# Shift products on two row tiles, set-up transfers from another engine, and other figures for the planner: a fused convolution and attention kernel

## The chip, the cores and the metric

The kernel runs on one core of a Trainium2 chip. The metric is the device time of one execution in microseconds; the kernel before took 4647.31 us (median of 3 runs, 4646.46 to 4648.82). The profiled execution spans 4642.4 us from its first to its last instruction.

A core has engines that work side by side, each through its own list of instructions in order: TensorE (PE in the profile, with its weight loads as PEld), VectorE (DVE), ScalarE (ACT), GpSimd (POOL) and SyncE (SP), which here only issues transfers. An instruction waits for semaphores that other engines and transfers raise; everything behind it on its engine waits with it.

## The reference

The input is 32 images of 96 channels and 56 x 56 pixels. Cut to what is computed:

```python
# layer 0, per image
h = relu(bn(w1 @ x))                  # 96 -> 576 channels
h = relu(bn(depthwise_conv3x3(h)))    # 9 taps a channel
x = x + bn(w2 @ h)                    # 576 -> 96 channels, and the residual
# layer 1, on 3136 tokens of 96 channels
u = relu(bn(layernorm(t) @ w1.T))     # 96 -> 192
X = fft(u)                            # over the tokens
y = ifft(relu(Re(X*c) + rb) + 1j * relu(Im(X*c) + ib)).real
t = t + bn(y @ w2.T)
t = t + ffn(layernorm(t))             # 96 -> 384 -> 96, rounded to fp8 and fp16
```

The batch norm behind `w2` is a scale, which the kernel multiplies into `w2`, and a shift of one number a channel, which has to be added to every token.

## The kernel before

**Stages.** An image is cut into two halves of 28 rows. For each half the 576 channels are worked as four blocks of 128 (`unit`, L598) and one of 64 (`last_channels`, L702). A unit expands on TensorE (L615), ScalarE evicts with Relu into `hs` (L625), begins the depthwise sum `acc` with one tap (L641) and makes one or two products (L657); VectorE adds the other taps (L668); GpSimd issues transfers that add the products to `acc` (L676); ScalarE finishes with a Relu (L685). `front` (L863) then brings everything to tokens: for 14 blocks of 112 tokens it sums in PSUM the transposed residual (L881, `ident`), the products with `w2T` over four channel blocks (L881), those of the last channels (L915), and the shift (L897). ScalarE evicts to `xt` (L928), and SyncE stores it (L937) for later. A layer norm on VectorE, a projection and a first transform follow (L974 to L1037); `mid` (L1067) does the Fourier mixing, and `back` (L1286) the inverse transform (L1324), the addition to the residual (L1329), the second norm, and the fp8 network (L1345 to L1458).

**The shift products.** `shb` holds the shift as three bf16 rows whose sum is the fp32 number, written four times side by side; `ones` is 3 x 112 ones. A product of `ones` and `shb` over a contraction of 3 adds the shift to four blocks of tokens at once. `front` walks two token halves t = 0, 1, which lie in two PSUM banks of the tile `pw`: for each t it issues four (or three) transposes and then one shift product. An image has four such pairs.

**The set-up.** `second` (L476) computes the shift on VectorE early in the kernel and sends each of the three rows to its partition of `shb` with a transfer issued by ScalarE (L484). `attention`, `mixer` and `ffn` prepare the other stages' constants; their square roots run on ScalarE (L432). SyncE issues the loads.

**The order.** No order is written out by hand. Each piece of work is a `step` with an engine, a cost, steps it comes after, buffers it takes and gives back, and a rank, the time at which it is due (`START`, `PACE`, `OFF`, `AT`). `Plan.emit` (L222) plays the engines forward on a clock of its own: an idle engine takes the due step of lowest rank whose inputs are ready and whose buffers are free. A step counts as done for others at its cost plus `late`, by engine from `LATE` (L163) or given. What comes out is the order of each engine's instructions, fixed at build time. `OFF[3]` is the rank of the finishing Relu within its unit.

**Fillers.** TensorE's clock falls when it idles. Where the planner's TensorE has nothing to do and was busy for less than 75% of the last 3.4 planned microseconds (`sparse`, L194), it issues a product of `ident` with itself into an unused part of `pw` (L1486), and charges 0.23 us. Such a product stands in TensorE's order like any other. An fp32 product shows as two passes in the trace.

**The buffers.** Three PSUM tiles `ps` serve all stages but `front`, which has `pw`; `acc` has seven buffers, `al` two, `product` and `hs` three each.

Of the kernel before, what the change touches and what calls it, by code (L numbers as in the profile page):

```python
# [34 lines left out]
BF16 = mybir.dt.bfloat16  # L35
# [6 lines left out]
C = 96  # L42
# [13 lines left out]
G = 7  # L56
# [74 lines left out]

SPARSE = 0.75
FILLER = 0.23

OFF = (-4.5, 0.5, 0.5, 8.5)
AT = (3.0, 0.5)

DOUBLE = (1, 3)
# [15 lines left out]
class Plan:  # L154
# [5 lines left out]

    LATE = {"PE": 0.23, "ACT": 0.18, "DVE": 0.15}  # L163
    WINDOW = 3.413
    LITTLE, FULL = 0.58, 0.965

# [55 lines left out]
    def emit(self):  # L222
        ready = {s.engine: [] for s in self.steps}
        idle = dict.fromkeys(ready, True)
        for s in self.steps:
            if not s.left:
                heapq.heappush(ready[s.engine], (s.rank, s.at, s))
        events, count, left = [(0.0, 0, None, None)], 1, len(self.steps)
        work = sum(s.engine == "PE" for s in self.steps)
        while events:  # L230
            now = events[0][0]
            while events and events[0][0] <= now:
                _, _, engine, s = heapq.heappop(events)
                if engine:
                    idle[engine] = True
                elif s:
                    for b in s.give:
                        self.free[b] += 1
                    for n in s.next:
                        n.left -= 1  # L240
                        if not n.left:
                            heapq.heappush(ready[n.engine], (n.rank, n.at, n))
            for engine, heap in ready.items():
                if not idle[engine]:
                    continue
                passed, wanted = [], set()
                while heap:
                    item = heapq.heappop(heap)
                    s = item[2]
                    short = {b for b in s.take if self.free[b] < s.take.count(b)}  # L250
                    if short or wanted.intersection(s.take):
                        wanted |= short
                        passed.append(item)
                        continue
                    for b in s.take:
                        self.free[b] -= 1
                    s.emit()
                    left -= 1
                    idle[engine] = False
                    cost = self.stretched(now, s.cost) if engine == "PE" else s.cost  # L260
                    if engine == "PE":
                        self.recent.append((now, now + cost))
                        work -= 1
                    late = self.moved(now, s.late) if isinstance(s.late, tuple) else s.late
                    heapq.heappush(events, (now + cost, count, engine, None))
                    heapq.heappush(events, (now + cost + late, count + 1, None, s))
                    count += 2
                    break
                for item in passed:
                    heapq.heappush(heap, item)  # L270
                if engine == "PE" and idle[engine] and work and now > 0 and self.sparse(now):

                    self.filler()
                    idle[engine] = False
                    cost = self.stretched(now, FILLER)
                    self.recent.append((now, now + cost))
                    heapq.heappush(events, (now + cost, count, engine, None))
                    count += 1
        assert not left, "a step waits for a buffer that nothing frees"
# [3 lines left out]
def tile_kernel(ctx: ExitStack, tc: tile.TileContext, d: dict, out: bass.AP):  # L283
# [19 lines left out]
    def cst(shape, name, dt=F32):  # L303
        return const.tile(shape, dt, name=name, tag=name)
# [29 lines left out]
    bd = cst([128, NK + 1], "bd")  # L334
    m2rb = cst([128, 2], "m2rb")

    shb = cst([3, 4, C], "shb", BF16)
    ones = cst([3, SK], "ones", BF16)
    w1q = cst([C, HF], "w1q", F8)
    w2q = cst([128, 3, C], "w2q", F8)  # L340
    b1q = cst([128, 3], "b1q")
# [134 lines left out]
    def second():  # L476
        g, v, b, m = given[0]
        s = scale_of(g, v, 128, C)
        sh, rest = tmp(1, C), tmp(1, C)
        shift_of(sh, b, m, s[0:1, :], rest)  # L480
        for n in range(3):
            part = tmp(1, 4 * C, BF16)
            nc.vector.tensor_copy(part.rearrange("p (q c) -> p q c", q=4), sh.unsqueeze(1).to_broadcast([1, 4, C]))
            nc.scalar.dma_start(out=shb[n : n + 1, :, :].rearrange("p q c -> p (q c)"), in_=part)  # L484
            nc.vector.tensor_sub(rest, sh, part[:, 0:C])
            sh = rest
        nc.vector.tensor_mul(w2T, w2T, s.unsqueeze(1).to_broadcast([128, NK + 1, C]))
# [66 lines left out]
    def pe(n, m, passes):  # L554
        return passes * max(0.855 * n, 0.88 * m) / 1000
# [307 lines left out]
    def front(img, s):  # L863
# [5 lines left out]
        def conv(i):  # L869

            def f():
                if i == 0:
                    if s == 0:

                        ydr[img] = dram.tile([2, NP, S, HA], F32, name="ydr", bufs=4)

                        tdr[img] = dram.tile([2, SK, RP * C], F32, name="tdr", bufs=4)
                    u["t"] = w1.tile([SK, RP, C], F32, name="xt")

                def add(n, t, src, rhs, rows=slice(None), **k):  # L880
                    nc.tensor.matmul(  # L881
                        u["pw"][0:SK, t, n % 4, 0:C],
                        lhsT=src[rows, (G * t + n) * SK : (G * t + n + 1) * SK],
                        rhs=rhs,
                        skip_group_check=True,
                        **k,
                    )

                if i % 4 == 0:
                    u["pw"] = pw[:, :, 0 : 4 * C].rearrange("p t (q c) -> p t q c", c=C)  # L890
                    n = min(4, G - i)

                    for t in range(2):
                        for m in range(i, i + n):
                            src = xs[img, s][:, x0 : x0 + W]
                            add(m, t, src, ident[0:C, 0:C], start=(m == i), stop=False, is_transpose=True)
                        nc.tensor.matmul(  # L897
                            u["pw"][0:SK, t, 0:n, 0:C],
                            lhsT=ones,
                            rhs=shb[:, 0:n, :],  # L900
                            start=False,
                            stop=False,
                            skip_group_check=True,
                        )
                for t in range(2):
                    for k in range(NK):
                        src = acc[img, s, k].rearrange("p r c -> p (r c)")
                        add(i, t, src, w2T[:, k, :], start=False, stop=False)
                if i in (3, 6):

                    last = acc[img, s, NK].rearrange("p r c -> p (r c)")
                    for n in range(i - i % 4, i + 1):
                        for t in range(2):
                            rows = slice(64 * t, 64 * t + 64)
                            nc.tensor.matmul(  # L915
                                u["pw"][0:SK, t, n % 4, 0:C],
                                lhsT=last[rows, n * SK : (n + 1) * SK],
                                rhs=w2T[rows, NK, :],
                                start=False,
                                stop=True,  # L920
                                skip_group_check=True,
                            )

            return f
# [15 lines left out]
        ev = []  # L940
        for i in range(G):
            n = min(4, G - i) if i % 4 == 0 else 0
            cost = pe(C, SK, 16) + n * (pe(C, SK, 2) + 0.13)
            if i in (3, 6):
                cost += pe(C, SK, 2 * (i % 4 + 1))
            t = [
                step(
                    "PE",
                    cost,
                    conv(i),  # L950
                    t,
                    ["pw"] * (i % 4 == 0) + ["xt"] * (i == 0) + ["ydr", "tdr"] * (s == 0 and i == 0),
                    (["acc"] * 4 + ["al"]) * (i == G - 1),
                )
            ]
            if i in (3, 6):
                a = i - i % 4
                ev.append(step("ACT", act((i + 1 - a) * 2 * C), evict(a, i + 1), t, [], ["pw"]))
# [327 lines left out]
    def back(img, h):  # L1286
# [41 lines left out]
        def add():  # L1328
            nc.vector.tensor_add(u["t"], u["t"], slots(u["ps"])[0:SK, 0:G, 0:C])  # L1329

        t = step("PE", pe(C, SK, 2 * G), spread, loads + [res], ["ps"], ["wd", "gd"])
        t = step("DVE", dve(G * C, 0.06), add, [t], [], ["ps"])
        t = norm(u, "f", G, SK, [t], True, NF, [])

# [219 lines left out]
```

## Time and profile before

| engine | busy us | share of the span | instructions |
|---|---|---|---|
| TensorE, products | 4496.0 | 97% | 35608 |
| TensorE, weight loads | 3351.9 | 72% | 35608 |
| VectorE | 4335.3 | 93% | 7053 |
| ScalarE | 4121.2 | 89% | 5390 |
| GpSimd | 339.9 | 7% | 397 |

| group | executions | busy us | mean ns |
|---|---|---|---|
| L668, taps, VectorE | 1664 | 2972.6 | 1793 |
| L615, expansion, TensorE | 2048 | 805.3 | 515 |
| L881, products with w2T, TensorE | 7168 | 792.8 | 264 |
| L1486, fillers, TensorE | 1862 | 268.2 | 283 |
| L897, shift products (n = 4), TensorE | 128 in the group | 46.7 | 365 |

The first table adds over the whole execution, so it averages a start, a steady state and a tail. The mean of a product in the second is a latency: products overlap, so busy time divided by the number (0.144 us for a pass of a filler) or, better, the distance of two starts says what one occupies. The transfers move 170 GB/s on average, and the granted TensorE clock is 0.994 over the execution.

### The profile page before, as it was taken

What the parts mean: (1) busy time and instruction counts of PE and PEld (TensorE: products, weight loads), DVE (VectorE), ACT (ScalarE), POOL (GpSimd) and SP (SyncE); (2) the same over time, 40 slices, a digit from 0 to 9 for tenths busy, and PEclk for the clock granted to TensorE, in tenths of its full rate; (3) what the DMA queues carried; (4) which work ended last, traced back from release to release, by engine and by line L of the source; (5) the groups of instructions that cost most, each with busy time, mean ns of one, the idle gap of its engine ahead of it and who ended that gap; (6) DMA issues with size and microseconds to landing.
All of it is one profiled execution on the core that took longest, in us unless ns stands there. A gap on an engine that the chain in (4) does not pass through costs nothing.

```text
span 4642.4 us, 89413 instructions
## 1 busy us (share of the span) xinstructions
PE 4496.0 (97%) x35608; PEld 3351.9 (72%) x35608; DVE 4335.3 (93%) x7053; ACT 4121.2 (89%) x5390; POOL 339.9 (7%) x397
## 2 busy tenths in 40 slices
PE   7999999999999999999999999999999999999998
PEld 4667777777777777777777777777777777777777
DVE  7899999999999999999999999999999999999956
ACT  4677999999999999999999999999999999999854
POOL 0100000000000000000000000000000000000000
PEclk8999999999999999999999999999999999999999
DMA  3577877767877777777767877767776867877753
GB/s 78 130 160 174 192 168 179 183 166 181 187 170 171 187 168 179 185 174 171 184 165 181 187 169 171 187 167 180 187 172 171 187 165 179 191 170 171 170 148 100
DMA packets 390902, 789.51 MB, mean 170 GB/s; under 512 B 135600, under 2 KB 236532, under 8 KB 390484
## 3 DMA queue, kind: packets, MB, share of 16 engines
q1 hardware_dynamic: 335028, 479.15, 37.0%
q0 software_dynamic: 55296, 304.64, 34.1%
q8 instruction: 280, 4.59, 0.4%
q14 instruction: 138, 1.13, 0.1%
q10 hardware_dynamic: 160, 0.01, 0.0%
HBM read 286.38 MB, written 192.68 MB: 103 GB/s over the span
## 4 chain that ended last, share of the span: by engine, by line
PE 56%; ACT 14%; DVE 14%; DMA 5%; issue 3%; SPq 0%; DVEq 0%; ACTq 0%; POOLq 0%
PE pw L881 14%; PE ps L615 9%; DVE acc L668 7%; PE ps L1118 4%; PE ps L1031 3%; PE ps L1000 3%; PE ps L1324 3%; ACT product L657 3%; DMA acc<-product 3%; PE ps L1216 2%; PE ps L753 2%; PE ps L1378 2%; PE pw L915 2%; PE ps L1423 2%; PE ps L717 1%
## 5 line engine op out<-in xcount | busy, mean ns | idle before, releaser
L668 DVE SCALAR_TENSOR_TENSOR acc<-hs,wdw,acc 128x1540 f32<-128x1540 f32 (+2 forms) x1664 | 2972.6, 1793 | 30.1 <-ACT acc L641 22.1
L615 PE MATMUL ps<-xs,w1T 96*128 96x406 f32 x2048 | 805.3, 515 | 18.7 <-ACT hs L625 13.7
L881 PEld LDWEIGHTS pw<-w2T,acc 128*112 128x112 f32 x7168 | 749.4, 178 | 63.6 <-issue 44.5
L881 PE MATMUL pw<-w2T,acc 128*112 128x96 f32 x7168 | 792.8, 264 | 0.5 <-ACT acc L685 0.5
L657 ACT ACTIVATE product<-hs,wdw 128x1568 f32<-128x1568 f32 (+1 forms) x384 | 609.4, 1588 | 17.8 <-DMA product<-product 17.4
L625 ACT ACTIVATE hs<-ps,b 128x812 f32<-128x812 f32 x512 | 478.7, 935 | 114.9 <-PE ps L615 85.1
L615 PEld LDWEIGHTS ps<-xs,w1T 96*128 96x128 f32 x2048 | 363.1, 191 | 251.2 <-issue 177.4
L676 POOL DMA_DIRECT2D acc<-product x256 | 224.6, 877 | 3317.1 <-DVE rf L854 936.7
L641 ACT ACTIVATE acc<-hs,bd,wdw 128x1568 f32<-128x1568 f32 x256 | 435.4, 1701 | 0.2
L685 ACT ACTIVATE acc<-acc 128x1568 f32<-128x1568 f32 x256 | 387.5, 1514 | 42.8 <-DMA acc<-product 42.6
L753 PE MATMUL ps<-hl,band 128*64 128x385 f32 (+3 forms) x3072 | 416.0, 495 | 0.2 <-ACT gc L1258 0.2
L1000 PE MATMUL ps<-watt,xnT 97*120 97x192 f32 x1792 | 334.1, 330 | 16.7 <-DVE V L1147 13.4
L1000 PEld LDWEIGHTS ps<-watt,xnT 97*120 97x120 f32 x1792 | 292.5, 183 | 71.9 <-issue 35.8
L1118 PEld LDWEIGHTS ps<-wb,yb 112*128 112x128 f32 x3528 | 296.6, 165 | 52.2 <-issue 16.0
L1390 ACT ACTIVATE h<-ps 128x784 f16<-128x784 f32 x384 | 315.5, 824 | 15.4 <-PE ps L1378 10.1
L1405 ACT ACTIVATE h<-h 128x784 fp8e5<-128x784 f16 x348 | 298.8, 859 | 34.0 <-DVE h L1396 33.7
L1118 PE MATMUL ps<-wb,yb 112*128 112x112 f32 x3528 | 321.2, 270 | 5.8 <-ACT h L1390 2.5
L1345 ACT ACTIVATE u<-tt,mf,rf 112x96 fp8e5<-112x96 f32 x812 | 315.2, 463 | 0.6 <-DVE mf L857 0.6
L753 PEld LDWEIGHTS ps<-hl,band 128*64 128x64 f32 (+1 forms) x3072 | 152.2, 134 | 209.9 <-issue 180.0
L1486 PE MATMUL pw<-ident 128*128 128x128 f32 x1862 | 268.2, 283 | 3.4 <-ACT xt L928 3.4
L1486 PEld LDWEIGHTS pw<-ident 128*128 128x128 f32 x1862 | 247.4, 197 | 24.9 <-issue 12.5
L1396 DVE TENSOR_SCALAR h<-h,b1q 128x784 f16<-128x784 f16 x384 | 160.2, 418 | 83.9 <-ACT h L1390 81.9
(170 smaller groups left out, 6788.0 us busy)
## 6 DMA issues: line engine op xcount, KB each, us to landing
acc<-product POOLq DMA_DIRECT2D x256, 784.0 KB, 7.3
product<-product POOLq DMA_DIRECT2D x128, 756.0 KB, 10.6
yb<-ydr SPq DMA_DIRECT2D x252, 294.0 KB
wd<-in_wd_dram SPq DMA_DIRECT2D x128, 349.1 KB
wb<-in_wb_dram SPq DMA_DIRECT2D x63, 686.0 KB
ydr<-ya SPq DMA_DIRECT2D x256, 168.0 KB
xs<-in_x_dram SPq DMA_DIRECT2D x64, 609.0 KB
tdr<-xt SPq DMA_DIRECT2D x64, 588.0 KB
```

The costliest lines, as they stand in the source:

```text
L615: nc.tensor.matmul(u[h][:, j, 0:QW], lhsT=w1T[:, 128 * k : 128 * (k + 1)], rhs=xs[img, s][0:C, at : at + QW], start=True, stop=True,)
L625: nc.scalar.activation(flat[:, 2 * h * QW : 2 * (h + 1) * QW].rearrange("p (j w) -> p j w", j=2), u[h][:, :, 0:QW], AF.Relu, bias=b1[:, k ...
L641: nc.scalar.activation(acc[img, s, k], u["hs"][:, o + up : o + up + R, :], AF.Identity, scale=weight(up, 0), bias=bd[:, k : k + 1],)
L657: nc.scalar.activation(u["p", dr][:, ra:rb, :], u["hs"][:, ra + o + dr : rb + o + dr, :], AF.Copy, scale=weight(dr, 0))
L668: nc.vector.scalar_tensor_tensor(dst, src, weight(dr, dc), dst, ALU.mult, ALU.add)
L685: nc.scalar.activation(acc[img, s, k], acc[img, s, k], AF.Relu)
L753: nc.tensor.matmul(pv[:, :, ca:cb], lhsT=band[rows, j, dc + 1, 64 * o : 64 * o + 64], rhs=H[rows, q : q + 7, ca + dc : cb + dc], skip_grou ...
L881: nc.tensor.matmul(u["pw"][0:SK, t, n % 4, 0:C], lhsT=src[rows, (G * t + n) * SK : (G * t + n + 1) * SK], rhs=rhs, skip_group_check=True, **k,
L1000: nc.tensor.matmul(pv[0:PK, q - a, 0:HA], lhsT=xnT[:, q, 0:PK], rhs=watt, start=True, stop=True,)
L1118: nc.tensor.matmul(o, lhsT=lhsT, rhs=u["wb"][:, G * s + q, :], start=True, stop=True)
L1390: nc.scalar.activation(u["h", c].rearrange("p (j w) -> p j w", j=2), u["H", c][:, :, 0:n], AF.Copy)
L1486: nc.tensor.matmul(pw[:, 0, 4 * C :], lhsT=ident, rhs=ident, start=False, stop=False, skip_group_check=True)
```

## The change

It does three things. The two shift products of a group are issued next to each other after the transposes of both halves, and take their operands from different rows: `ones` and `shb` become 67 rows high with a second copy at rows 64 to 66, so that the product of t = 0 uses the row tile at 0 and that of t = 1 the one at 64. The transfers that fill `shb` are now six and are issued by GpSimd. And the planner gets other figures: TensorE results count as later (0.30 in place of 0.23, and 0.40 for the spread at L1324), the shift products as cheaper, the finishing Relu is due half a unit of rank earlier, and no filler is issued before its clock shows 15.

```diff
+FIRST = 15.0
-OFF = (-4.5, 0.5, 0.5, 8.5)
+OFF = (-4.5, 0.5, 0.5, 8.0)
...
-    LATE = {"PE": 0.23, "ACT": 0.18, "DVE": 0.15}
+    LATE = {"PE": 0.3, "ACT": 0.18, "DVE": 0.15}
...
-                if engine == "PE" and idle[engine] and work and now > 0 and self.sparse(now):
+                if engine == "PE" and idle[engine] and work and now > FIRST and self.sparse(now):
...
-    shb = cst([3, 4, C], "shb", BF16)
-    ones = cst([3, SK], "ones", BF16)
+    shb = cst([67, 4, C], "shb", BF16)
+    ones = cst([67, SK], "ones", BF16)
...
-            nc.scalar.dma_start(out=shb[n : n + 1, :, :].rearrange("p q c -> p (q c)"), in_=part)
+            for o in (n, 64 + n):
+                nc.gpsimd.dma_start(out=shb[o : o + 1, :, :].rearrange("p q c -> p (q c)"), in_=part)
...
                         for m in range(i, i + n):
                             src = xs[img, s][:, x0 : x0 + W]
                             add(m, t, src, ident[0:C, 0:C], start=(m == i), stop=False, is_transpose=True)
+                    for t in range(2):
+                        rows = slice(64 * t, 64 * t + 3)
                         nc.tensor.matmul(
                             u["pw"][0:SK, t, 0:n, 0:C],
-                            lhsT=ones,
-                            rhs=shb[:, 0:n, :],
+                            lhsT=ones[rows, :],
+                            rhs=shb[rows, 0:n, :],
...
-            cost = pe(C, SK, 16) + n * (pe(C, SK, 2) + 0.13)
+            cost = pe(C, SK, 16) + n * (pe(C, SK, 2) + 0.07)
...
-        t = step("PE", pe(C, SK, 2 * G), spread, loads + [res], ["ps"], ["wd", "gd"])
+        t = step("PE", pe(C, SK, 2 * G), spread, loads + [res], ["ps"], ["wd", "gd"], late=0.4)
```

## The prediction

> **What bounds the kernel now.** I read the engine totals first, then the steady state in windows of 140 us, then the waits of each engine there, and last the time line of the first 110 us. The totals name no single bound: TensorE and VectorE are both above 90%.
> ```profile
> PE 4496.0 (97%) x35608; PEld 3351.9 (72%) x35608; DVE 4335.3 (93%) x7053; ACT 4121.2 (89%) x5390; POOL 339.9 (7%) x397
> PE 56%; ACT 14%; DVE 14%; DMA 5%; issue 3%; SPq 0%; DVEq 0%; ACTq 0%; POOLq 0%
> ```
> The second line is the chain that ended last: TensorE holds 56% of it. Two neighbouring windows of the steady state (busy time of PE, weight loads, DVE, ACT, POOL, then the granted clock):
> ```profile
> 1970.00:2110.00 140.00, 137.08 (x1098) 102.25 (x1097) 132.78 (x215) 130.32 (x173) 10.59 (x12) 1.00 0.77 180
> 2110.00:2250.00 140.00, 137.53 (x1085) 100.89 (x1083) 134.29 (x218) 131.24 (x174) 10.48 (x12) 1.00 0.72 174
> ```
> TensorE is occupied 98% of each. But part of that is filler, products that nobody reads (L1486). The same two windows for that line alone:
> ```profile
> 1970.00:2110.00 140.00, 6.83 (x46) 6.09 (x46) 1.00 0.77 180
> 2110.00:2250.00 140.00, 3.55 (x22) 3.15 (x22) 1.00 0.72 174
> ```
> An fp32 product is two passes in the trace, so that is 23 and 11 fillers, 0.30 us each, 5.2 us per image on average. Issue times of the residual store (L937) put one image at 139.0 us in the steady state, and images alternate between 135 and 143 us with their fillers. VectorE is busy 267.1 of 280 us, hence 132.6 us per image, and idles 6.4. What it waits for, 150 to 4400 us:
> ```profile
> DVE tt L1329 <- PE ps L1324: 55.8, 86, 1.7
> DVE h L1396 <- ACT h L1390: 51.1, 47, 2.9
> DVE sta L825 <- ACT xt L928: 21.3, 15, 5.6
> ```
> The first is a TensorE result taken too early by the planned order, and the other two are ScalarE copies of TensorE results: VectorE has the most real work, and its idle time comes from TensorE being late. Now the start, ScalarE's time line and then VectorE's:
> ```profile
> 16.77 0.27 ACT L432 ACTIVATE V<-V 128x96 f32<-128x96 f32 x1
> 30.10 2.35 ACTq L484 DMA_DIRECT2D shb<-yb  x3
> 32.50 1.77 ACT L625 ACTIVATE hs<-ps,b 128x812 f32<-128x812 f32 x2 [15.46 <-DMA shb<-yb]
> ```
> ```profile
> 21.48 0.64 DVE L487 TENSOR_TENSOR w2T<-w2T,V 128x480 f32<-128x480 f32 x1
> 36.02 25.99 DVE L668 SCALAR_TENSOR_TENSOR acc<-hs,wdw,acc 128x1485 f32<-128x1485 f32 x15 [13.91 <-ACT acc L641]
> ```
> ScalarE stands 15.5 us at three 0.8 KB transfers whose data VectorE had ready at 21.3. In the built program each of them also waits for an earlier SyncE load that holds the same completion semaphore, and those loads trickle until 30. Behind them in ScalarE's order stand the evictions of hs and the first begin (L641), and VectorE's first tap waits 13.9 us for that.
>
> **What the Trainium skill says.** "TensorE: Matmul & The Clock Gate", Part 3, says that matmuls on different row tiles run concurrently, with a span of about one duration plus 4 ns per further tile, and that a weight load overlaps a running matmul only when its row group differs. The trace of before agrees with the second half: its two shift products share rows 0 to 2, and each takes its full slot. It agrees with the first half too: 28 products of L1204, 64 rows in turns on two row tiles, occupy 1.54 us (time line at 2026.67), while 28 of L1216 over all 128 rows, with the same output, occupy 2.74 (436.35): a pair costs 1.1 slots in place of 2. Part 1 of that page says that an idle TensorE falls to half clock and is released by sustained work; the trace agrees, with a granted clock of 0.76 in the first 50 us and 1.00 later. "DMA: Bandwidth & Descriptors", Latency and other measured facts, gives about 1 us to first byte for transfers issued by GpSimd against 0.6 for ScalarE; here an issue takes POOL 0.86 us (L676) and ScalarE 0.5 (L484), so the direction agrees. "Perfetto Trace Analysis", Tensor Engine Instruction, says that the ends of TensorE's records are estimated; that is why I use starts for the slots below.
>
> **The change, part by part.**
> (1) Shift products. The trace has, for n = 3, starts at 2015.69 (shift), 2015.95 (next transpose), 2016.34 (shift), 2016.60 (first product of w2T): 0.26 us a slot, and 0.29 for n = 4 (2069.10 to 2069.39). After, the eight (or six) transposes come first and the two shifts stand next to each other on row tiles 0 and 64, in two banks. Saved per pair: between 0 (they don't overlap) and 0.29 (the second is free); at L1204's ratio 0.9 x 0.275 = 0.25, of which I take 0.2, since a pair alone has no run of products on both sides. Four pairs an image: 0.8 us of TensorE.
> (2) Fillers. The built program has 931 before and 691 after; per steady image 23 and 11 in turns (17) before, 10 after. 7 x 0.30 = 2.1 us an image of TensorE. They fall because the planner's clock thinks shifts cheaper (0.07 in place of 0.13 us) and its steady order now repeats every image in place of every two.
> (3) Later TensorE results (0.30 in place of 0.23, 0.40 for the spread of L1324). This reorders all engines. Mean wait at L1329 is 55.8 / 86 = 0.65 us, so 0.17 later doesn't clear it: 86 x 0.17 = 15 us at most. Other evictions move by 0.07, and the finishing Relu half a rank earlier. I count nothing for these by themselves; what hides them is that VectorE waits are mostly TensorE lateness, counted in (1) and (2).
> (4) Set-up transfers on GpSimd, six in place of three, and they wait for VectorE alone. GpSimd is idle from 3.5 to 45.4 us, so 6 x 0.9 = 5.4 us there is hidden, and their reader (L897) comes at 108 us. ScalarE's order loses the stop. VectorE's first tap is then set by the work ahead of it, L487, which ends at 22.1 and depends on loads that don't move: 36.0 - 22.2 = 13.8 us earlier. Also the root of the attention set-up now stands early in ScalarE's order; before it cost VectorE 5.3 us (L308, 62 to 67). Against this, that scale needs a load which lands near 26 us, and two taps bring VectorE just there, so 1 to 3 us return as new waits.
> (5) No fillers before planned time 15. The 24 fillers hold TensorE from 7.84 to 14.37, ahead of the first expansion. Without them it starts near 9.5 but on a cold clock, 16 passes in up to 11 us in place of 5.6; begin then comes at about 20.7, still before 22.2. Hidden: nothing gained or lost beyond (4).
> Sum at the start: 13.8 + 5.3 - 4 (the new waits and 2 us of reserve for a cold start) = 15 us, and every later VectorE instruction moves with it, since VectorE was busy 94% from 36 us on.
> Sum in the steady state: TensorE loses 2.9 us an image. If all of it reached the period, 139.0 would fall to 136.1. Not all will: VectorE needs 132.6 and its idle time would have to halve. The alternating images give a measure. Windows with 11 fillers have VectorE at up to 135.1 of 140, and 132.6 x 140 / 135.1 = 137.4; the shift adds some. I take 137.0, that is 2.0 us an image, over 29 images at full load: 58 us.
> The tail (4400 on) is a chain of latencies with idle TensorE; its fillers fall from 211 to 166 and hide in waits. Nothing.
> Total: 4647 - 15 - 58 = 4574 us.
>
> **Rivals.**
> A. TensorE alone is the bound and the whole relief passes: 4647 - 15 - 29 x 2.9 = 4548. With the lateness of L1329 gone as well, another 15 to 25, and 4525. For it: 56% of the chain, real TensorE idle of 2.6 us an image. Against: VectorE would reach over 97%.
> B. VectorE and ScalarE in their planned order are the bound, and fillers merely fill what would be waits: only the start is gained, 4632, or with 0.5 us an image 4618. For it: fillers are placed where the planner has TensorE idle. Against: on the chip TensorE is 98% occupied, so the planner's idle places no longer exist.
> C. Slower. The new order meets another wait: results planned later mean longer chains through the three PSUM buffers and the nine buffers of acc and al, or adding DMAs that ScalarE waits for (L685, 36.5 us in the steady state) come to lie worse. With 1.0 us more an image and the start gained: 4647 - 15 + 29 = 4661. For it: every engine's order moves, and 29 images repeat one bad place. Against: no buffer is removed, and the work itself shrinks.
>
> **How the numbers follow.** My forecast, with 50%: 4574. Rival A 22%, B 21%, C 7%. Range: from 4510, where A and the shorter waits add up, to 4636, where B gains only part of the start. That leaves out about C and the far end of A. Faster by over 0.2% (below 4638): 0.91; within: 0.03; slower: 0.06.
>
> **What would show it.** In the trace after: ScalarE without the stop at 17 to 32 us and the first tap near 22; the two shift products starting less than 0.1 us apart; filler busy time of 1380 passes near 200 us in place of 268; a spacing of images near 137, even from image to image; VectorE at 96 to 97% of the steady windows; the wait of L1329 below 40 us. If VectorE's waits grow in total or ScalarE's wait for adding DMAs does, C is at work; if the spacing stays at 139 although TensorE's busy share falls, it is B.

## The result and the profile after

| kernel | median us | runs | ratio to before | 95% interval |
|---|---|---|---|---|
| before | 4648.07 | 4 | 1 | |
| changed | 4586.31 | 4 | 0.9867 | 0.985 to 0.9884 |

The change takes 62 us off; 73 were forecast. The totals of the changed kernel and the shares of its chain:
```profile
PE 4405.4 (96%) x35128; PEld 3296.1 (72%) x35128; DVE 4330.6 (94%) x7053; ACT 4114.5 (90%) x5390; POOL 340.7 (7%) x403
PE 48%; ACT 22%; DVE 16%; DMA 8%; issue 4%; POOLq 0%; ACTq 0%; POOL 0%; SPq 0%; DVEq 0%
```
TensorE does 91 us less, VectorE nearly the same work, and part of the chain has moved from TensorE (56 to 48%) to ScalarE (14 to 22%) and to the adding transfers. The start, ScalarE's first begin and then VectorE's first tap:
```profile
16.74 1.69 ACT L643 ACTIVATE acc<-hs,bd,wdw 128x1568 f32<-128x1568 f32 x1
...
18.47 3.59 DVE L670 SCALAR_TENSOR_TENSOR acc<-hs,wdw,acc 128x1485 f32<-128x1485 f32 x2 [2.26 <-ACT acc L643]
```
The first tap starts at 18.5 us in place of 36.0. The shift pair in TensorE's time line, both products in one row (x2), and what starts next:
```profile
2044.85 0.37 PE L902 MATMUL pw<-shb,ones 3*112 3x384 bf16 x2
2045.15 1.81 PE L883 MATMUL pw<-w2T,acc 128*112 128x96 f32 x16
```
Both together take 0.30 us, the slot of one before; their starts are 3 ns apart. Waits in the steady state (total, times, longest), for VectorE to 4400 us as shown of before, then for TensorE and ScalarE to 4340:
```profile
DVE rf L853 <- ACT sdf L837: 53.6, 56, 3.1
...
DVE h L1401 <- ACT h L1395: 20.4, 27, 3.6
...
DVE tt L1334 <- PE ps L1329: 2.5, 3, 1.9
```
```profile
PE ps L1005 <- DVE V L1152: 58.2, 28, 2.1
```
```profile
ACT acc L687 <- DMA acc<-product: 80.7, 38, 5.1
```
The three waits of VectorE shown of before fall from 128.2 us in all to 33.2 (the third is now L827, 10.3). New ones stand in their place: VectorE for a root on ScalarE, TensorE once an image for VectorE's combine, ScalarE for the adding transfers (36.5 before). And the steady windows differ among themselves (PE, weight loads, DVE, ACT, POOL, granted clock):
```profile
990.00:1130.00 140.00, 136.15 (x1077) 101.34 (x1075) 133.20 (x215) 130.10 (x173) 10.46 (x12) 0.98 0.73 176
1130.00:1270.00 140.00, 135.96 (x1075) 101.17 (x1075) 133.11 (x215) 130.03 (x173) 10.45 (x12) 0.98 0.72 176
...
2390.00:2530.00 140.00, 136.48 (x1122) 102.05 (x1121) 136.39 (x218) 133.11 (x176) 10.45 (x12) 1.00 0.74 180
```
In the window at 1.00 VectorE works 136.4 of 140 us, in those at 0.98 only 133.1 and 133.2. All 28 windows from 430 us on say the same: 134.9 to 137.4 in the fourteen at 1.00, 133.1 to 133.4 in the five at 0.98. The first two windows show the new wait with its consequence. TensorE's time line there, and the same stretch cut into pieces of 3.41 us:
```profile
1069.19 0.61 PE L1491 MATMUL pw<-ident 128*128 128x128 f32 x4
1071.94 2.27 PE L1005 MATMUL ps<-watt,xnT 97*120 97x192 f32 x6 [2.14 <-DVE V L1152]
```
```profile
1068.51:1071.92 3.41, 1.29 (x10) 1.10 (x8) 3.41 (x4) 3.41 (x9) 0.00 (x0) 0.97 1.02 180
1071.92:1075.33 3.41, 3.39 (x8) 2.74 (x9) 3.41 (x3) 1.51 (x4) 0.00 (x0) 0.50 0.39 148
1075.33:1078.75 3.42, 3.42 (x19) 2.57 (x18) 3.42 (x5) 3.42 (x5) 0.00 (x0) 0.53 0.00 0
1078.75:1082.16 3.41, 3.41 (x38) 2.38 (x36) 2.08 (x4) 2.88 (x2) 0.00 (x0) 1.00 0.00 0
```
TensorE does two fillers, waits 2.14 us, and then runs at half clock for almost 7 us: 8 passes and 19 where the next piece has 38.

To place gains I use SyncE's issue times of the residual store (L937, or the same line in each kernel). The third store comes at 248.4 us before and at 223.6 after; from the 14th to the 62nd store, 24 images, one image takes 139.3 before and 138.0 after. So the start gave 25 us at the third store, of which the next image lost 12 (the fifth store is 12.2 us earlier) and 8 are left at the 14th, the steady state gave 31 over those 24 images, and the tail, from the last store to the end of the span, fell from 180.9 to 169.1 us.

### The profile page after: what moved, and what is told of

Its sections match the earlier page's. It is cut to its first block, busy times and chain, and to the rows that moved or that the text cites. A ratio compares the mean times of both kernels' runs of the same rounds, so it can differ in the third digit from the quotient of the medians.

```text
span 4584.2 us, 88412 instructions
## 1 busy us (share of the span) xinstructions
PE 4405.4 (96%) x35128; PEld 3296.1 (72%) x35128; DVE 4330.6 (94%) x7053; ACT 4114.5 (90%) x5390; POOL 340.7 (7%) x403
## 4 chain that ended last, share of the span: by engine, by line
PE 48%; ACT 22%; DVE 16%; DMA 8%; issue 4%; POOLq 0%; ACTq 0%; POOL 0%; SPq 0%; DVEq 0%
PE pw L883 11%; DVE acc L670 10%; PE ps L617 9%; DMA acc<-product 7%; PE ps L1005 4%; PE ps L1123 4%; PE ps L755 3%; PE ps L1036 3%; ACT product L659 3%; ACT hs L627 2%; ACT acc L687 2%; ACT acc L643 2%; PE ps L1329 2%; ACT h L1410 2%; ACT h L1395 2%
## 5 line engine op out<-in xcount | busy, mean ns | idle before, releaser
L617 PE MATMUL ps<-xs,w1T 96*128 96x406 f32 x2048 | 819.8, 523 | 24.6 <-ACT h L1395 16.7
L687 ACT ACTIVATE acc<-acc 128x1568 f32<-128x1568 f32 x256 | 387.5, 1514 | 90.9 <-DMA acc<-product 85.1
L1005 PE MATMUL ps<-watt,xnT 97*120 97x192 f32 x1792 | 345.3, 337 | 60.9 <-DVE V L1152 59.6
L1005 PEld LDWEIGHTS ps<-watt,xnT 97*120 97x120 f32 x1792 | 299.0, 187 | 125.3 <-DVE V L1152 65.6
L1152 DVE SCALAR_TENSOR_TENSOR sb<-ps,cw,V 128x784 f32<-128x784 f32 x192 | 197.0, 1026 | 31.1 <-ACT V L1136 25.4
L1018 ACT ACTIVATE z<-ps 120x768 f32<-120x768 f32 (+1 forms) x256 | 182.3, 725 | 44.9 <-PE ps L1005 44.9
L1036 PE MATMUL ps<-z,wa 56*64 56x384 f32 (+1 forms) x2048 | 217.5, 496 | 0.3
```

The source lines that it names most:

```text
L617: nc.tensor.matmul(u[h][:, j, 0:QW], lhsT=w1T[:, 128 * k : 128 * (k + 1)], rhs=xs[img, s][0:C, at : at + QW], start=True, stop=True,)
L687: nc.scalar.activation(acc[img, s, k], acc[img, s, k], AF.Relu)
L1005: nc.tensor.matmul(pv[0:PK, q - a, 0:HA], lhsT=xnT[:, q, 0:PK], rhs=watt, start=True, stop=True,)
```

## The experiments

Each kernel was timed against before on the same chip; before took 4646.8 to 4649.4 us on the chips used, and medians from different chips are compared with that much doubt. "Order of before" means the order that the planner makes of its figures of before.

**1. The transfers alone.** Edit to the kernel before:
```diff
-            nc.scalar.dma_start(out=shb[n : n + 1, :, :].rearrange("p q c -> p (q c)"), in_=part)
+            nc.gpsimd.dma_start(out=shb[n : n + 1, :, :].rearrange("p q c -> p (q c)"), in_=part)
```


> The kernel before with one edit: the three set-up transfers of the shift are issued by GpSimd. The order of all engines stays as before but for these three. Theory S (the parts of the prediction add up, the start gives 15 to 25 us of which the first images give some back): first tap of VectorE near 22 us in place of 36, the first store of a residual about 13 us earlier, and 4648 - 14 = 4634 us. Rival F (the planner's figures make the gain, the start is given back by the third image): 4646, no difference that can be told.


Measured: 4627.34 us, ratio 0.9961 (0.9947 to 0.9974). VectorE's time line:
```profile
20.50 0.64 DVE L487 TENSOR_TENSOR w2T<-w2T,V 128x480 f32<-128x480 f32 x1
21.07 25.97 DVE L668 SCALAR_TENSOR_TENSOR acc<-hs,wdw,acc 128x1485 f32<-128x1485 f32 x15
```
The first tap is 15 us earlier, the third store 18.4 and the last 19.1, at an unchanged 139.3 us an image. The tap now follows the multiplication of `w2T` at once, as step (4) of the prediction had it. So the start's gain is kept to the end, 20 us, and the theory that it is given back falls for this order; the changed kernel's loss of 12 us in its second image belongs to its figures.

**2. Pairs without a second row tile.** Edit to the changed kernel:
```diff
-                        rows = slice(64 * t, 64 * t + 3)
+                        rows = slice(0, 3)
```


> The changed kernel with one edit: both shift products of a pair use rows 0 to 2, so they stand next to each other as in the changed kernel but share a row tile. Same order on every engine. Theory S: the second product takes its slot of 0.26 to 0.30 us again, 128 pairs x 0.28 = 36 us of TensorE, of which two thirds reach the end: 4586 + 24 = 4610 us. Rival F (TensorE's relief doesn't pass through, since VectorE and ScalarE hold the order): 4586 +- 4.


Measured: 4602.99 us, ratio 0.9912 (0.9898 to 0.9926), 17 us later than the changed kernel; 138.7 us an image in the profiled execution, which was the longest of four (4614.81). TensorE's time line:
```profile
2050.59 0.82 PE L883 MATMUL pw<-ident,xs 96*112 96x96 f32 x8
2051.34 0.53 PE L902 MATMUL pw<-shb,ones 3*112 3x384 bf16 x2
2051.80 1.81 PE L883 MATMUL pw<-w2T,acc 128*112 128x96 f32 x16
```
The pair takes 0.46 us here, against 0.30 on two row tiles and 0.59 for two products apart before. So standing next to each other already saves 0.13, besides what it saves at the transposes (experiment 3), and the second row tile 0.16; the expectation had put the whole slot on the row tile.

**3. The planner's figures back.** The changed kernel with all figures of before:
```diff
-FIRST = 15.0
-OFF = (-4.5, 0.5, 0.5, 8.0)
+FIRST = 0.0
+OFF = (-4.5, 0.5, 0.5, 8.5)
...
-    LATE = {"PE": 0.3, "ACT": 0.18, "DVE": 0.15}
+    LATE = {"PE": 0.23, "ACT": 0.18, "DVE": 0.15}
...
-            cost = pe(C, SK, 16) + n * (pe(C, SK, 2) + 0.07)
+            cost = pe(C, SK, 16) + n * (pe(C, SK, 2) + 0.13)
...
-        t = step("PE", pe(C, SK, 2 * G), spread, loads + [res], ["ps"], ["wd", "gd"], late=0.4)
+        t = step("PE", pe(C, SK, 2 * G), spread, loads + [res], ["ps"], ["wd", "gd"])
```


> The changed kernel with all of the planner's figures of before (TensorE results 0.23 later and no 0.40 for the spread, finishing Relu at 8.5, shift cost 0.13, fillers from time 0), so the planned order and the 931 fillers of before, with the transfers on GpSimd and the paired shift products of the changed kernel. Theory S: transfers 14 and pairs 24 us are gained, 4648 - 38 = 4610 us, and the figures are worth the other 24. Rival F: 4634 to 4646, the figures are worth 50 or more.


Measured: 4595.16 us, ratio 0.9889 (0.9876 to 0.9903). Neither forecast had it: it is 15 us faster than theory S said. This kernel differs from experiment 1 by the pairs, and gains 32 us on it: 138.2 us an image in place of 139.3, so 1.1 us. One group (n = 4) from its first transpose to its first product with `w2T`, in experiment 1 and then here:
```profile
2048.67 0.49 PE L881 MATMUL pw<-ident,xs 96*112 96x96 f32 x4
2049.09 0.36 PE L897 MATMUL pw<-shb,ones 3*112 3x384 bf16 x1
2049.39 0.54 PE L881 MATMUL pw<-ident,xs 96*112 96x96 f32 x4
2049.86 0.36 PE L897 MATMUL pw<-shb,ones 3*112 3x384 bf16 x1
2050.16 1.81 PE L881 MATMUL pw<-w2T,acc 128*112 128x96 f32 x16
```
```profile
2039.85 0.82 PE L883 MATMUL pw<-ident,xs 96*112 96x96 f32 x8
2040.60 0.37 PE L902 MATMUL pw<-shb,ones 3*112 3x384 bf16 x2
2040.90 1.81 PE L883 MATMUL pw<-w2T,acc 128*112 128x96 f32 x16
```
The group takes 1.49 us and then 1.05, one of n = 3 takes 1.24 and then 0.85. The shift products give 0.29 and 0.26 of that and the transposes, no longer parted by a shift, the other 0.14. Two groups of each an image make 1.7 us of TensorE, of which 1.1, two thirds, reach the image time. And this kernel differs from the changed kernel by the figures alone: they are worth 9 us, and the two intervals overlap. By stores: with the figures the third store is 10 us earlier, the second image loses what that gained and more (from the third to the 14th store 753.5 us in place of 731.2), the steady state is the same (138.0 and 138.2), and the tail is 12 us shorter (169.1 and 181.0).

**4. Fillers for the new wait.** The changed kernel with five more fillers ahead of the second projection group where the planner had set one between the two groups (`gap` starts as an empty list):
```diff
         def project(i, a, b):
             def f():
+                if i and gap:
+                    for _ in range(5):
+                        filler()
+                gap.clear()
...
     def filler():
+        gap.append(1)
```


> The changed kernel with five more fillers (1.5 us) in each image, put ahead of the second group of the projection (L1005) wherever the planner had set a filler between its two groups. There TensorE now waits 2.1 us for VectorE's combine (L1152), and in images where this falls into one activity window the granted clock is 0.5 for the two windows after it (1071.9 to 1078.7 us). Theory K (the half clock is what costs: such images take 140.0 us and the others 136.5 to 137.5): the clock stays at 1.00, all images near 137, 4586 - 20 = 4566 us. Rival W (the wait for VectorE costs, the clock is a bystander): within 4 us of 4586. Rival P (the fillers delay TensorE where VectorE was in time): 4586 + 28 x 0.5 = 4600.


Measured: 4562.46 us, ratio 0.9819 (0.9806 to 0.9833). It has 836 fillers in place of 691 and is 24 us faster than the changed kernel, clear of both intervals. The same windows as above:
```profile
990.00:1130.00 140.00, 137.31 (x1103) 101.53 (x1102) 136.15 (x218) 132.62 (x176) 10.45 (x12) 1.00 0.73 177
1130.00:1270.00 140.00, 136.45 (x1110) 101.08 (x1110) 135.06 (x219) 130.64 (x173) 10.46 (x12) 1.00 0.73 176
```
The clock is 1.00, an image takes 137.1 us, and VectorE works 135 to 136. What the projection waits for, a `ps` buffer that the combine has to free, comes no sooner: from 150 to 4340 us TensorE still waits 29.8 us there, and the added fillers are busy for 29.8 us in the steady state, together the 58.2 of the wait above. The granted clock of the execution rises from 0.988 to 0.994, and 0.006 of 4586 us is 28. So the 24 us are the half clock and not the wait.

**5. Eight fillers there.** Edit to experiment 4:
```diff
-                    for _ in range(5):
+                    for _ in range(8):
```


> As e4_fill_gap, with eight more fillers (2.4 us) in place of five in the same place. The wait they fill is 2.1 us long in the changed kernel. Theory K: five already hold the clock, so three more only delay TensorE by what exceeds the wait, 28 x (2.4 - 2.1) = 8 us at least and 28 x 0.9 = 25 us at most: 4570 to 4588. Rival Q (more filler holds the clock in further places): 4562 or less.


Measured: 4566.41 us, ratio 0.9827 (0.9813 to 0.984). The medians are 4 us apart, within the intervals, and an image takes 137.1 us in both. So more filler there gains nothing more that can be told; whether it costs nothing or the expected 8 us is inside the noise.

**6. TensorE results at 0.23 again.** Edit to the changed kernel, the 0.40 kept:
```diff
-    LATE = {"PE": 0.3, "ACT": 0.18, "DVE": 0.15}
+    LATE = {"PE": 0.23, "ACT": 0.18, "DVE": 0.15}
```


> The changed kernel with one figure back: TensorE results count as 0.23 late instead of 0.30 (the 0.40 for the spread stays). The built order has 737 fillers, and one filler between the two projection groups in each image in place of two. Theory L (the later results make the steady order of VectorE better and at the same time make the wait at L1005): VectorE's wait for ScalarE's root (L853, 53.6 us from 150 to 4340) falls, its wait at L1334 comes back to 25 us or more, TensorE's wait at L1005 falls below 30 us, and the two roughly cancel: 4590 +- 8 us. Rival M (0.30 is the figure that pays, the rest of the figures cost): 4605 us or more. Rival N (0.30 only does harm here): 4575 or less.


Measured: 4599.19 us, ratio 0.9897 (0.9884 to 0.9911). 13 us more than the changed kernel, at the edge of the intervals and 1 us beyond what theory L allowed. Its directions hold: the wait at L1005 falls from 58.2 to 32.8 us (below 30 was expected) and the root's from 53.6 to 42.1. But L1334 comes back to 8.4 only, and VectorE's wait at L1401 rises from 15.1 to 70.9 (both to 4340 us). By the stores this figure works both ways: from the third to the 14th store 736.3 us in place of 753.5, so the second image's loss is gone (118.1 us from the third to the fifth store in place of 131.4), but then 139.0 us an image in place of 138.0, and a tail of 178.7 in place of 169.1.

**7. The shift cost at 0.13 again.** Edit to the changed kernel:
```diff
-            cost = pe(C, SK, 16) + n * (pe(C, SK, 2) + 0.07)
+            cost = pe(C, SK, 16) + n * (pe(C, SK, 2) + 0.13)
```


> The changed kernel with one figure back: the planner charges 0.13 us a block for the shift pair in place of 0.07. The built order has 740 fillers in place of 691. Rival R (the cost figure removes fillers and that is its worth): 49 fillers x 0.3 = 15 us of TensorE, 4596 +- 4. Theory O (a figure acts only through the order, in which waits move and the image time falls on or off a multiple of the activity window): any sign, within 15 us of 4586, and the change is explained by the share of images at half clock.


Measured: 4594.82 us, ratio 0.9888 (0.9875 to 0.9902): 8 us more, intervals overlapping. The forecast by fillers (4596) fits, and so does "any sign within 15". But the half clock doesn't explain the change, as theory O had it: fewer windows are below 1.00 (8 of 28, the changed kernel 14), and yet the time is longer. Nor does the fit speak for the fillers, which experiment 11 prices at far less. From the third to the fifth store it takes 120.2 us, so the second image's loss is gone here too.

**8. The finishing Relu at 8.5, with the filled wait.** Edit to experiment 4:
```diff
-OFF = (-4.5, 0.5, 0.5, 8.0)
+OFF = (-4.5, 0.5, 0.5, 8.5)
```


> As e4_fill_gap, with the finishing Relu back at rank 8.5. In the changed kernel ScalarE waits 80.7 us at L687 (150 to 4340 us) for transfers that add products, against 36.5 before. Theory D (the earlier rank puts the Relu ahead of the end of its transfer, which stops ScalarE): that wait falls below 50 us, and since ScalarE is 94% busy a third of it is gained: 4562 - 14 = 4548 us. Rival E (the wait at L687 stands where ScalarE would wait anyway, and an earlier Relu helps TensorE's products): 4562 or more, whatever the wait does.


Measured: 4561.26 us, ratio 0.9813 (0.9799 to 0.9826), the same as experiment 4. ScalarE's wait at L687 goes from 83.8 to 73.0 us only. Theory D falls on both counts: the earlier rank isn't what made most of that wait, and shortening it by 11 us gave nothing that can be told.

**9. Fillers of half the width, in the order of before.** Edit to experiment 3:
```diff
-        nc.tensor.matmul(pw[:, 0, 4 * C :], lhsT=ident, rhs=ident, start=False, stop=False, skip_group_check=True)
+        nc.tensor.matmul(
+            pw[:, 0, 4 * C : 4 * C + 64], lhsT=ident, rhs=ident[:, 0:64], start=False, stop=False, skip_group_check=True
+        )
```


> As e3_old_figures (planned order of before), with each of the 931 fillers 64 columns wide in place of 128, so about half as long. Theory C (step 2 of the prediction: a filler costs TensorE its whole time, and images alternate between 135 and 143 us because of their 23 and 11 fillers): 17 x 0.13 = 2.2 us an image less, two thirds of it gained, 4595 - 40 = 4555 us, and the alternation shrinks. Rival V (fillers stand where TensorE would wait, and shortening them only lengthens waits): 4595 +- 5 with the clock kept, or later where the clock falls to half in a window.


Measured: 4617.2 us, ratio 0.9932 (0.992 to 0.9945). The fillers' group (busy time, mean ns), the first two windows, and the first of them in experiment 3:
```profile
L1491 PE MATMUL pw<-ident 128*128 128x64 f32 x1862 | 266.1, 285 | 3.3 <-ACT xt L933 3.3
```
```profile
0.00:150.00 150.00, 130.96 (x735) 95.62 (x736) 121.54 (x164) 76.61 (x72) 15.72 (x30) 0.83 0.43 90
150.00:430.00 280.00, 264.95 (x1950) 198.57 (x1949) 251.47 (x274) 198.81 (x219) 24.13 (x28) 0.93 0.70 158
```
```profile
0.00:150.00 150.00, 126.45 (x786) 89.37 (x787) 128.90 (x169) 82.72 (x80) 16.58 (x31) 0.90 0.47 97
```
The edit missed its aim: half the columns take nearly the same time, 266.1 us where the full ones take 264.6 in experiment 3, and 138.8 against 150.2 from 430 to 4340 us, at full clock. The weight loads of these products are busy for 133.9 us there in both; that they are what keeps the time up is likely, not shown. What did change is the clock, 0.83 and 0.93 in these windows against 0.90 and 0.98 in experiment 3. Of the 15 us between the two profiled executions 11 are lost by the third store and 4 in the tail: the steady state takes 138.0 us an image, against 138.2. On the cost of fillers this run says nothing.

**10. Each filler twice, in the order of before.** Edit to experiment 3:
```diff
     def filler():
+        for _ in range(2):
-        nc.tensor.matmul(pw[:, 0, 4 * C :], lhsT=ident, rhs=ident, start=False, stop=False, skip_group_check=True)
+            nc.tensor.matmul(pw[:, 0, 4 * C :], lhsT=ident, rhs=ident, start=False, stop=False, skip_group_check=True)
```


> As e3_old_figures, with each filler issued twice, which can't lower the clock. Theory C: 17 x 0.3 = 5 us an image more, so 4595 + 29 x 5 = 4740 us. Rival V: the first fillers of a wait are free and the doubled ones are not wholly: an image of 23 (46) fillers loses 1 to 3 us and one of 11 (22) less, 4610 to 4650; the start adds some 7 us, since the 24 fillers ahead of the first expansion are doubled too.


Measured: 4683.46 us, ratio 1.0073 (1.006 to 1.0085), 139.7 us an image in place of 138.2. The fillers' busy time rises from 150.2 to 258.5 us between 430 and 4340 us, 3.9 us an image (the second of two takes less than the 0.3 reckoned), and 1.5 of it reach the image time. The rest went into waits. The theory of full cost gave 4740; the measured time lies above the rival's 4650 too. The third store, 17 us later, and the tail, 25 us longer, are part of that.

**11. Every second filler left out in the steady state, in the order of before.** Edit to experiment 3; `halves` grows by one with each half image that `front` begins:
```diff
     def filler():
+        if 6 <= len(halves) < 60:
+            passed.append(1)
+            if len(passed) % 2:
+                return
```


> As e3_old_figures (planned order of before), with every second filler left out from the fourth image to the thirtieth: 697 fillers in place of 931, 12 and 5 an image in place of 23 and 11, about the number of the changed kernel, and full width. Start and tail keep theirs. Doubling the fillers (e14_double_filler) cost 1.5 us an image for 5.1 us of added filler, which is 29% of it, so the first halves are not dearer than that. Theory C (step 2: a filler costs its whole time): 8.5 x 0.3 = 2.6 us an image less, 4595 - 26 x 2.6 = 4527 us. Rival V (fillers stand in waits): at most 29% of that, 4575 to 4599, if the clock holds at 1.00; above 4599 if it falls in some windows.


Measured: 4590.23 us, ratio 0.9879 (0.9863 to 0.9896), 138.0 us an image with the clock at 1.00. The steady state (430 to 4340 us) of experiments 3, 10 and 11:
```profile
430.00:4340.00 3910.00, 3833.07 (x30820) 2855.51 (x30819) 3781.34 (x6058) 3675.10 (x4870) 297.89 (x340) 1.00 0.75 178
```
```profile
430.00:4340.00 3910.00, 3869.77 (x31466) 2936.15 (x31459) 3739.94 (x6000) 3646.30 (x4825) 294.31 (x336) 1.00 0.74 177
```
```profile
430.00:4340.00 3910.00, 3802.43 (x30386) 2808.62 (x30384) 3782.32 (x6054) 3676.64 (x4875) 297.71 (x340) 1.00 0.75 178
```
The fillers alone (PE, weight loads), in experiment 3 and then here:
```profile
430.00:4340.00 3910.00, 150.20 (x988) 133.90 (x988) 1.00 0.75 178
```
```profile
430.00:4340.00 3910.00, 88.54 (x520) 77.78 (x520) 1.00 0.75 178
```
The number of fillers is 697, close to the changed kernel's 691. Their time falls by 62 us, TensorE's busy time by 31, and VectorE's stays within 1 us: 2.2 us an image of filler taken away give 0.2 us of image. Images still alternate between 134 and 141 us, with 5 and 12 fillers in place of 11 and 23, so the alternation isn't theirs.

**12. Fillers from the start, with the filled wait.** Edit to experiment 4:
```diff
-FIRST = 15.0
+FIRST = 0.0
```


> As e4_fill_gap, with fillers from planned time 0 on, so that 17 more stand in the first image's order, most of them ahead of the first expansion. Theory H (step 5: they hold TensorE ahead of the first expansion but the clock is then warm, and the first tap waits for other work): first tap later by 0 to 4 us, total 4562 to 4566. Rival G (the start is on the path, and TensorE at 9.2 in place of 14.4 us brings the first tap to 18.5): 4567 or more.


Measured: 4561.62 us, ratio 0.9807 (0.9794 to 0.9821). The first expansion begins at 14.6 us and the first tap, again right behind the multiplication of `w2T`, at 22.3 in place of 18.8 in experiment 4. The third store comes at 224.3 us in both, and the time is the same. So the start fillers do hold up the first tap, but those microseconds are gone by the third store.

## Why the prediction came out right, and which steps were not

The time was in the range and near its middle, and that is luck in good part: the terms were wrong, and their errors cancelled. Forecast were 15 us for the start, 16 for the pairs and 42 for the fillers (0.8 and 2.1 of 2.9 us an image, two thirds of each, 29 images). Measured are 20, 32 and, for all the planner's figures together, 9.

- **The start** was put at 15 us and is 20 (experiment 1). The stop of ScalarE was read rightly, and so was what would hold the first tap without it: the multiplication of `w2T`, at 21.1 us where 22.2 was forecast. What was wrong is why that comes so late. It doesn't wait for loads until 22 us but for a root that stands behind the first eviction in ScalarE's order, and so behind the expansion and the start fillers. Without those fillers the planner sets the root ahead of the evictions, the multiplication ends at 16.2 us, and the first tap waits for begin, at 18.5. So they were not hidden at the first tap, as step (5) said, but at the end they are (experiment 12). The six transfers took GpSimd 0.49 us each to issue (L486), not 0.9. The two issue times that the prediction sets beside the page's latencies are another thing than the time to the first byte, which no run here shows.
- **The shift pairs** were mis-sized in cost: 0.2 us of TensorE a pair was put down, 0.8 an image, and it is 0.4 and 1.7 (experiment 3). That two thirds of it would pass came true: 1.1 us an image, 32 us in all. The pair itself saves a whole slot, 0.29, the upper bound named; I went below the 0.25 of L1204's ratio without need. The other 0.14 comes from the transposes and was not thought of: by their starts, a transpose takes 0.08 us ahead of another transpose and 0.18 ahead of a shift. That the shift products of before each take a full slot shows nothing about weight loads on the same rows, for transposes stand between them. Experiment 2 comes nearer, with 0.46 us for two neighbours on the same rows.
- **The fillers**, 2.1 us an image and the larger part of the 58 us, are the step that failed. Between 430 and 4340 us their busy time did fall, from 149.1 to 103.1 us, 1.7 us an image. But it is mostly time that TensorE would have waited: taking 2.2 us an image away gives 0.2 (experiment 11), adding 3.9 costs 1.5 (experiment 10). The measure that I took for it, images of 135 and 143 us with 11 and 23 fillers, was a coincidence of order: it stays when the fillers are halved, and by the stores of the other half image the same images take about 138 and 140 us. Rival B had this point, though not the pairs.
- **The later results** were counted as nothing, with 15 us at most for L1329's wait. That wait vanished (55.8 to 2.5 us), so the bound was wrong: the new order clears more than the shift of one due time; how it does so was not taken apart. But the sum of all figures is only 9 us, since the new order has a wait of TensorE for VectorE and a half clock behind it, which experiment 4 prices at 24, and the images from the third to the 14th store take 22 us more than in the order of before. Rival C's mechanism was at work, at a size that didn't turn the sign; it named the PSUM buffers, and the new wait is for one of them, but it put none on the clock. The clock is cited in the prediction from "TensorE: Matmul & The Clock Gate", Part 1 (idle falls to half clock, sustained work releases it): the traces agree, with 0.50 after a wait of 2.14 us, though the page gives an idle window of about 3.4 us and here TensorE was busy for 1.29 of the 3.41 us. Except for the start, the prediction didn't ask what fewer fillers do to it.

Of the signs named ahead: the first tap near 22 came at 18.5; the two shift products start 3 ns apart, within the 0.1 us named; filler busy time near 200 us is 207.1; the wait of L1329, below 40 us, is 2.5; ScalarE's wait for the adding transfers, the sign of rival C, did grow, from 36.5 to 80.7; VectorE at 96 to 97% of the steady windows holds (3769.0 of 3910 us from 430 to 4340, 96.4%); the spacing near 137, even from image to image, is 138.0 and between 135.6 and 140.0, without the alternation.

When the wait at L1005 brings the half clock can be read from the trace. In all the kernels here the granted clock changes only on a grid of 3.413 us. In the changed kernel, 26 of the 28 waits shown above last 2.06 us or more. The 13 of them that begin between 0.53 and 0.76 of a step of this grid have no half clock behind them; the other 13 have it, for one step or two, beginning between 0.4 us before the wait's end and 1.8 us after it. So an image that takes a whole number of steps meets the clock at the same place again: the half clock begins at 1071.7, 1211.7 and 1351.6 us, 139.95 apart, which is 41 steps.

What stays open: why the changed kernel's second image loses 12 us. By the stores it is the figures' doing, and it goes when either of two is taken back, the 0.30 (experiment 6) or the 0.07 (experiment 7). The longest piece of the chain there is a transfer that adds a product (17.5 us at 351.6); no run took it apart. The 0.40 for the spread at L1324 was not tried alone either.

## What to carry to other kernels

An engine that is 98% busy with filler in it may still be waiting: count how much of the filler stands where the engine would wait anyway, by leaving some out or doubling it, before its time is counted as a gain. A transfer issued from a compute engine's list can stop that engine: here ScalarE stood 15.5 us at three transfers whose data were ready at 21.3 us. An idle engine can issue them; GpSimd did from 19.3 to 21.1 us (experiment 1), as soon as the data were there. That a shared completion semaphore made the stop was read from the built program; no run tested it. And after any change of order, look at the granted clock in small windows: one wait of 2 us an image cost 24 us of 4586 through the clock, and five useless products in that wait took it back.

## What the runs showed that I had not expected

Two products with a contraction of 3 cost 0.59 us apart, 0.46 next to each other on one row tile, and 0.30 on two (n = 4). A filler of 64 columns occupies TensorE nearly as long as one of 128 (266.1 and 264.6 us for 1862 passes, experiments 9 and 3) but holds the clock less: 0.83 against 0.90 in the first 150 us, though TensorE is busy for 131.0 us of them against 126.5. So busy time in the trace alone doesn't tell the clock.
